# Asking for the sum so far three units ahead instead of two, in a mixture-of-experts tail

## The chip, the cores and the metric

The kernel runs on one core of one Trainium2 chip. The time is device microseconds of that core; the median of several runs is compared. Below, PE is the tensor engine, DVE the vector engine, ACT the scalar engine, POOL the GpSimd engine, SP the sync engine. Matrix results land in PSUM, everything else that the engines work on lies in SBUF, and the large tensors lie in DRAM.

## The reference

Four residual blocks on 4096 tokens (4 x 1024) of width 1024, each gated by a tanh of an input: a block-quantized projection of the context, an 8-bit/ternary linear layer, an 8-head attention over feature blocks, and a mixture of eight low-rank experts. The change lies in the last block:

```python
norm = jnp.maximum(jnp.linalg.norm(x, axis=-1, keepdims=True), 1e-12)
routing_weights = softmax(x / norm @ router_w)            # 8 experts
rw, selected_experts = jax.lax.top_k(routing_weights, 2)
rw = rw / jnp.sum(rw, axis=-1, keepdims=True)
combine = sum(one_hot(selected_experts, 8) * rw[..., None], axis=1)
for e in range(8):
    out = out + combine[:, e, None] * (x @ Wa[e] @ Wb[e])  # 1024 -> 128 -> 1024
x = x + tanh(g_ffn[1]) * out                               # x inside is the layer norm of x
```

So each token gets two expert terms, one from the lower-numbered and one from the higher-numbered of its two experts, on top of its own row.

## The kernel before

Up to about 1660 us the kernel computes the first three blocks and the routing, with the tokens in 32 tiles of 128. The last block works on another tiling. Tokens are sorted into lists by expert, once by the lower and once by the higher expert of each token, and every list is cut into **units** of 128 tokens of one expert (`class Unit`). There is room for 38 units of each kind (`NS` = 38, `NU` = 76): units 0 to 37 are those of the lower expert, units 38 to 75 those of the higher. Room is taken for the worst split of tokens over experts, so the last units of a list, and of each expert, hold padding. A padding row's index lies out of bounds, and such a row is not transferred.

A unit takes these steps:

- `gather` (POOL, L1395): an indirect DMA fetches the 128 rows of the unit, 1028 values each (the row, its two expert weights, and the scale and offset of its layer norm). Lower down this is called the row gather.
- `normalize` (ACT, L1414), `transpose` (PE L1431 into two PSUM tiles, ACT L1435 copies both out as hgT).
- `choose` and `fetch` (DVE, L1440, L1444, L1451): read the expert's number and copy its two weight matrices to fixed places of `arena["w"]`, two places for each matrix.
- `down` (PE L1460, then ACT L1465 copies the 128x128 result as ygT) and `up` (PE L1470, two halves of 512 into a PSUM tile of which there are two).
- `finish` (DVE, L1485): og = weight x product + base, and then `send` (POOL, L1495): an indirect DMA stores the 128 rows of og. For og there are three buffers.

For a unit of the lower expert, the base is the token's own row, and the store goes to a DRAM tensor `x4`. For a unit of the higher expert, the base is the **sum so far**, the rows that the lower half stored in `x4`; they are fetched by one more indirect DMA on POOL, `resume` (L1407), and og goes to the output. A token's two units can be anywhere, so the first `resume` has to wait until every store of the lower half has landed. Because of that, units 38 and 39 are "held": their `finish` writes only weight x product (L1482), and `settle` (L1491) adds the sum so far and stores when unit 40 is at its finish.

`resume` has four buffers, by the unit's number modulo 4: two of a pool's tag `vT` for remainders 0 and 1, and slots 2 and 3 of `arena["x"]` for the others.

Everything in this stage runs in the order in which it is written, on each engine separately (`manual_schedule` for PE, DVE, ACT and POOL). The loop at the end of the kernel issues, for unit s: row gathers that run up to 14 units ahead, `down` of s+1, `choose` and `transpose` of s+2, `normalize` of s+3, `fetch` of s+1, `up` and `finish` of s, and then `resume` of s+2. On each engine a unit's steady order is thus:

- PE: down s+1, transposes s+2, up s
- ACT: ygT s+1, two copies hgT s+2, normalize s+3
- DVE: first weight copy (s+2), second weight copy (s+1), og s
- POOL: row gather of s+14 (until unit 62, when there are no more rows to fetch), store s, resume s+2

SP issues nothing in this stage. All indirect DMAs go through one queue of POOL, and the eight counters that tell of their landing are used in turn.

Of the kernel before, what the change touches and what calls it, by code (L numbers as in the profile page):

```python
# [53 lines left out]
def flamingo_kernel(  # L54
# [63 lines left out]
    NS = (NTOK + (NE - 1) * (P - 1)) // P  # L118
    NU = 2 * NS
# [45 lines left out]
    with ExitStack() as s1:  # L165
# [79 lines left out]
        class Media(Fp8):  # L245
# [11 lines left out]
            def range(self):  # L257
                g = self.group
                nc.vector.tensor_reduce(
                    g.column(g.rmax, self), self.c.rearrange("p (b k) -> p b k", k=P), AX.X, ALU.max,  # L260
                    apply_absolute_value=True,
                )
                if self is g.tiles[-1]:
                    g.turn()
# [32 lines left out]
        class Group:  # L297
# [17 lines left out]
            def begin(self):  # L315
                self.rmax = self.tiny("rmax")
# [1183 lines left out]
    us = [Unit(s) for s in range(NU)]  # L1500
# [4 lines left out]
    def tail(before):  # L1505

        t = NT - 1
        listed, last = routes[t - 2], routes[t - 1]
        before.cross()
        for name in ("w", "x"):  # L1510
            arena[name] = w2.tile([P, 4, XW], F32, tag="sq", name=f"arena_{name}")

        nc.gpsimd.memset(arena["x"][:, 3, D - 12 : XW], 0.0)
        for i in (3, 7):
            nc.gpsimd.memset(eT_x[:, i, D - 12 : XW], 0.0)
        attended(t - 1, 1)
        last.moments()
        for u in us[3:6]:
            u.gather()
        attend(t, 0, 0)  # L1520
        listed.count()
        attend(t, 0, 1)
        last.normalize()
        listed.enlist()
        listed.send()
        attend(t, 0, 2)
        last.transpose(0)
        last.take(0)
        attend(t, 0, 3)
        last.transpose(1)  # L1530
        last.take(1)
        attended(t, 0)
        attend(t, 1, 0)
        last.logits()
        us[0].normalize()
        last.collect()
        attend(t, 1, 1)
        last.total()
        last.softmax()
        us[1].normalize()  # L1540
        last.choose()
        last.classify()
        us[6].gather()
        attend(t, 1, 2)
        attend(t, 1, 3)
        us[0].choose()
        us[1].choose()
        us[0].fetch()
        attended(t, 1)
        routes[t] = Route(t)  # L1550
        routes[t].moments()
        us[0].transpose()
        last.count()
        last.enlist()
        last.send()
        us[1].transpose()
        us[0].down()
        us[2].normalize()
        routes[t].normalize()

    def hooks(s):

        h = [nothing] * 4
        r = routes[NT - 1]
        if s == 0:
            h[3] = lambda: (r.transpose(0), r.take(0))
        elif s == 1:
            h[1] = lambda: (r.transpose(1), r.take(1))
            h[3] = lambda: (r.logits(), r.collect())
        elif s == 2:  # L1570
            h[1] = lambda: (r.total(), r.softmax())
            h[2] = r.choose
            h[3] = r.classify
        elif s == 3:
            h[1] = lambda: (r.count(), r.enlist(), r.send())
            h[2] = rest.measure
        elif s == 4:
            h[1] = rest.place
            h[3] = rest.find
        elif s == 6:  # L1580
            h[1] = rest.list
        return h
# [52 lines left out]
    with tc.manual_schedule(engines=ORDERED):  # L1635
        intro()
        for t in range(NT):
            for mb in range(NB):
                now = step(t, mb, now)
                e = (t - NT + 2) * NB + mb - 3  # L1640
                if 0 <= e < NE:
                    nc.sync.dma_start(wb_sb[:, e, :], wb[e])
                if t == NT - 1:
                    if mb == 2:
                        early.measure()
                    elif mb == 3:
                        early.place()
                    elif mb == 5:
                        early.find()
                    elif mb == 7:  # L1650
                        early.list()
                        for u in us[0:3]:
                            u.gather()
        tail(now)
        done = 7
        for s, u in enumerate(us):
            begin, first, second, end = hooks(s)
            begin()

            ahead = min(s + 7, EARLY) if s < 7 else min(s + 14, done + 2)  # L1660
            for a in us[done:ahead]:
                a.gather()
            done = max(done, min(ahead, NU))
            if s == NS:
                u.resume()
                us[s + 1].resume()
            if s + 1 < NU:
                us[s + 1].down()
            first()
            if s + 2 < NU:  # L1670
                us[s + 2].choose()
                us[s + 2].transpose()
            second()
            if s + 3 < NU:
                us[s + 3].normalize()
            if s + 1 < NU:
                us[s + 1].fetch()
            u.up()
            if s == NS + 2:
                us[NS].settle()  # L1680
                us[NS + 1].settle()
            u.finish()
            if NS <= s < NU - 2:
                us[s + 2].resume()
            end()


# [36 lines left out]
```

## Time and profile before

The median of three runs is 2027.59 us (2027.41 to 2028.21). The profile is one further execution.

| | |
|---|---|
| time of the profiled execution | 2021.54 us |
| its span, first to last instruction | 2019.8 us |
| mean granted TensorE clock | 0.987 |
| PE, DVE, ACT, POOL busy over the span | 1919.0, 1642.1, 1448.3, 598.9 us |
| units 0 to 37, from the first up-product | 1664.5 to 1840.1 us |
| units 38 to 75 | 1840.1 to 2014.4 us |
| one undisturbed unit on PE | 4.38 us |
| `resume` on POOL (38 of them) | 1.0 us each, median |
| `send` on POOL | 1.2 us each, median |
| og on DVE | 1.28 us each |

In a timeline each row is the start in us, the duration in us, engine, line, operation, what is written from what is read; the brackets at its end hold the time that the engine stood idle before, and what ended it. An indirect DMA's duration on POOL is that of its issue alone; the data lands later. "remote" is a release that the profile can't name. "issue" is time for which it shows no wait. PE's ends are modelled, so starts are compared here.

### The profile page before, as it was taken

The numbers are of one execution on the slowest core, as the hardware profiler recorded it, in microseconds if no ns is written. First come the engines' busy times: TensorE is split into PE (matmuls) and PEld (weight loads), VectorE is DVE, ScalarE is ACT, GpSimd is POOL, SyncE is SP. The second block draws the span as 40 slices with busy tenths as digits, with TensorE's granted clock in tenths as the row PEclk, the third lists the DMA queues.
The fourth block names the chain that finished last, engine by engine and source line by source line (L and its number), as shares of the span: only waits on it lengthen the run. The fifth ranks groups of instructions, "written<-read, shape, count | busy, mean of one in ns | idle before, by whom it ended". The sixth has DMA issues, their size and how long they took to land.

```text
span 2019.8 us, 25358 instructions
## 1 busy us (share of the span) xinstructions
PE 1919.0 (95%) x7379; PEld 1016.3 (50%) x7411; DVE 1642.1 (81%) x3381; ACT 1448.3 (72%) x2458; POOL 598.9 (30%) x915
## 2 busy tenths in 40 slices
PE   3899999999789999999999999999999989999998
PEld 3644444444334444444444444444444447777676
DVE  8799888866778999999999999999999856555555
ACT  8988888998567777777777777777777645555554
POOL 2232323344300212121211111111111136546664
PEclk9899999999899999999999999999999999999999
DMA  4243233252376777777777777777777856746885
GB/s 156 95 158 124 94 115 105 103 199 95 145 206 159 181 195 179 197 180 196 184 192 183 193 182 193 183 193 181 195 184 182 223 162 213 268 169 201 288 301 175
DMA packets 125328, 359.89 MB, mean 178 GB/s; under 512 B 30647, under 2 KB 38839, under 8 KB 125190
## 3 DMA queue, kind: packets, MB, share of 16 engines
q1 hardware_dynamic: 95670, 273.87, 49.6%
q0 software_dynamic: 29520, 84.39, 12.5%
q8 instruction: 60, 0.98, 0.2%
q14 instruction: 78, 0.64, 0.1%
HBM read 166.18 MB, written 75.61 MB: 120 GB/s over the span
## 4 chain that ended last, share of the span: by engine, by line
PE 82%; DVE 6%; ACT 4%; issue 4%; POOL 3%; DMA 1%; POOLq 0%; another core or an unknown queue 0%; DVEq 0%; ACTq 0%
PE av L994 21%; PE sc L914 21%; PE mm L427 18%; PE f L875 5%; PE dn L1460 5%; PE up L1470 4%; PE pt_hmT L1042 1%; PE ptx L414 1%; PE pt_hg_pt L1431 1%; PE pt_hg_acc L1431 1%; PE pq L1054 1%; ACT e L923 1%; DVE nmax L919 1%; POOL a_all L133 1%; PE ptq L867 1%
## 5 line engine op out<-in xcount | busy, mean ns | idle before, releaser
L914 PE MATMUL sc<-kv,q 128*128 128x512 f32 x1024 | 489.6, 601 | 3.9 <-ACT q L902 2.1
L994 PE MATMUL av<-eT_x,vT 128*128 128x512 f32 x1008 | 477.3, 596 | 2.3 <-issue 0.4
L923 ACT ACTIVATE e<-sc,nmax 128x1024 f32<-128x1024 f32 x256 | 285.1, 1113 | 229.1 <-DVE nmax L919 226.2
L427 PE MATMUL mm<-wq,hT 128*128 128x512 f32 x960 | 423.7, 598 | 6.1 <-DVE x1s L447 6.1
L919 DVE TENSOR_REDUCE nmax<-sc 128x1 f32<-128x1024 f32 x256 | 311.8, 1218 | 44.0 <-PE sc L914 43.8
L929 ACT ACTIVATE e<-e,rden 128x1024 f32<-128x1024 f32 x256 | 294.2, 1149 | 58.9 <-DVE rden L926 55.2
L942 DVE STREAM_TRANSPOSE sq<-e 128x1024 f32<-128x1024 f32 x252 | 310.8, 1233 | 0.1
L994 PEld LDWEIGHTS av<-eT_x,vT 128*128 128x128 f32 x1008 | 189.3, 190 | 231.3 <-issue 227.4
L427 PEld LDWEIGHTS mm<-wq,hT 128*128 128x128 f32 x960 | 180.5, 192 | 218.2 <-issue 205.0
L914 PEld LDWEIGHTS sc<-kv,q 128*128 128x128 f32 x1024 | 185.5, 191 | 188.0 <-issue 176.1
L1460 PEld LDWEIGHTS dn<-hgT,arena_w 128*128 128x128 f32 x1216 | 148.3, 193 | 50.2 <-issue 35.9
L1460 PE MATMUL dn<-hgT,arena_w 128*128 128x128 f32 x1216 | 151.5, 278 | 12.2 <-ACT hgT L1435 7.7
L133 POOL TENSOR_TENSOR rstd_c<-ve_c,neg_half 128x1 f32<-128x1 f32 x31 | 17.6, 568 | 461.8 <-DVE nrm L1069 405.2
L1470 PE MATMUL up<-arena_w,ygT 128*128 128x512 f32 x304 | 143.0, 593 | 0.0
L875 PE MATMUL f<-wb_sb 128*128 128x512 bf16 x465 | 115.4, 379 | 4.2 <-DVE y L883 1.4
L1465 ACT COPY ygT<-dn 128x128 f32<-128x128 f32 x76 | 20.1, 265 | 127.0 <-PE dn L1460 92.8
L225 ACT ACTIVATE y_x<-x,off_x,up_x 128x128 f32<-128x128 f32 x256 | 101.5, 480 | 1.1 <-POOL off_x L396 1.1
L237 ACT ACTIVATE hd<-q_x,down_x 128x128 f32<-128x128 bf16 x256 | 78.1, 388 | 26.2 <-DVE mu_a L363 17.5
L875 PEld LDWEIGHTS <-wb_sb 128*128 128x128 bf16 x496 | 48.5, 98 | 81.6 <-issue 29.7
L1144 POOL DMA_INDIRECT lists<-token,slot x64 | 66.6, 1041 | 67.6 <-DVE slot L1137 57.0
L133 POOL TENSOR_TENSOR y<-ve_d,neg_half 128x1 f32<-128x1 f32 x32 | 18.3, 572 | 213.4 <-issue 162.2
L133 POOL TENSOR_TENSOR a_all<-va,neg_half 128x1 f32<-128x1 f32 x32 | 46.9, 1465 | 97.9 <-DVE va L467 97.9
(297 smaller groups left out, 2940.9 us busy)
## 6 DMA issues: line engine op xcount, KB each, us to landing
eT_x<-sq SPq DMA_DIRECT2D x1008, 128.0 KB
x<-y SPq DMA_DIRECT2D x32, 514.0 KB
c<-in_ctx_t_dram SPq DMA_DIRECT2D x32, 512.0 KB
x<-in_x_dram SPq DMA_DIRECT2D x32, 512.0 KB
x<-x1s SPq DMA_DIRECT2D x32, 512.0 KB
y<-x SPq DMA_DIRECT2D x32, 512.0 KB
kv<-in_ctx_dram SPq DMA_DIRECT2D x32, 512.0 KB
vT<-in_ctx_t_dram SPq DMA_DIRECT2D x32, 512.0 KB
```

Source lines behind the costliest of these rows:

```text
L133: nc.gpsimd.tensor_tensor(dst, src, exponent, ALU.pow)
L225: nc.scalar.activation(self.y[:, cols(k)], src[:, cols(k)], AF.Identity, bias=bias[:, k : k + 1], scale=scale[:, k : k + 1],)
L427: nc.tensor.matmul(self.pm[:, hf * HALF : (hf + 1) * HALF], self.hT[:, k, :], wq[:, k, :], start=(k == 0), stop=(k == NB - 1),)
L875: nc.tensor.matmul(po, self.qT[:, k, :], w0T[:, k, cols], start=(k == 0), stop=(k == NB - 1),)
L914: nc.tensor.matmul(sc[:, halves(nh)], qs[t][:, mb * P : (mb + 1) * P], kv[:, halves(nh)], start=True, stop=True,)
L919: nc.vector.tensor_reduce(nmax, sc, AX.X, ALU.max, negate=True)
L923: nc.scalar.activation(self.e, sc, AF.Exp, bias=nmax, accum_out=self.den)
L929: nc.scalar.activation(self.e, self.e, AF.Copy, scale=self.rden)
L942: nc.vector.transpose(sq[:, :, :, j, :], self.e.rearrange("p (k q a) -> p q k a", k=NB, q=4))
L994: nc.tensor.matmul(out_ap, vTs[t][:, k, :], weights, start=(k == 0), stop=(k == NB - 1))
L1460: nc.tensor.matmul(po, self.wa[:, k, :], self.hT[:, k, :], start=(k == 0), stop=(k == NB - 1),)
L1470: nc.tensor.matmul(po[:, halves(hf)], self.yT, self.wb[:, halves(hf)], start=True, stop=True)
```

## The change

Each `resume` of the higher half is issued one unit sooner. Unit 38 begins with three of them (38, 39, 40), where it had two; after its finish comes 41. After unit 39 there is none. After unit 40, when `settle` has read the buffers of 38 and 39, come 42 and 43, and from then on unit s is followed by s+3. The buffers and their number stay the same, so in the steady state `resume` of s+3 fills the buffer that unit s−1 has read.

```diff
@@ the loop over units
             if s == NS:
-                u.resume()
-                us[s + 1].resume()
+                for a in us[s : s + 3]:
+                    a.resume()
             if s + 1 < NU:
                 us[s + 1].down()
             first()
@@
                 us[NS].settle()
                 us[NS + 1].settle()
             u.finish()
-            if NS <= s < NU - 2:
-                us[s + 2].resume()
+
+            for a in {NS: (3,), NS + 1: (), NS + 2: (2, 3)}.get(s, (3,) if s > NS else ()):
+                if s + a < NU:
+                    us[s + a].resume()
             end()
```

On POOL the order of instructions becomes, from unit 38 on (before: 38, 39, 40, row gather, 41, row gather, three stores, 42, row gather, store 41, 43, row gather, store 42, 44 and so on, where a bare number is a resume): 38, 39, 40, 41, two row gathers, stores of 38, 39 and 40, 42, 43, row gather, store 41, 44, row gather, store 42, 45 and so on. The number and the size of the DMAs are unchanged, and so are the orders of PE, DVE, ACT and SP.

## The prediction

> **What bounds the kernel now.** I read four views: the busy table by stage, the waits of the last stage, its timeline unit by unit, and the chain that ended last. The change touches only the second half of the expert stage (units 38 to 75), so the first question is how much time that half can give back.
>
> The busy table by stretches (us of the stretch; then busy us and instruction count of PE, PEld, DVE, ACT, POOL; then granted clock, DMA share, GB/s), cut where the higher expert's units begin (1840) and where the row gathers of its units run out (1966):
>
> ```profile
> core 0: us, PE busy (x) PEld busy (x) DVE busy (x) ACT busy (x) POOL busy (x), PEclk, DMA share, GB/s
> ...
> 1660.00:1840.00 180.00, 175.20 (x1136) 135.97 (x1135) 105.51 (x165) 98.67 (x162) 99.04 (x98) 1.00 0.61 205
> 1840.00:1966.00 126.00, 117.79 (x730) 89.99 (x729) 67.02 (x80) 65.48 (x104) 83.41 (x79) 0.99 0.83 281
> 1966.00:2020.00 54.00, 46.70 (x284) 34.88 (x282) 27.58 (x33) 23.62 (x39) 26.17 (x24) 0.97 0.53 179
> ```
>
> TensorE is busy 117.8 of 126 us even in the stretch with the heaviest DMA. A unit costs it 4.38 us: its up-products start at 1938.77, 1943.14 and 1947.52. Subtracting 4.376 us from every step between up-products of units 38 to 74 leaves 12.3 us lost, in three places. (a) Units 42 and 43: 0.80 + 5.27 us (up-products at 1853.23, 1858.41, 1868.06). (b) Units 50 and 53: 2.83 + 2.23 us (1894.32 to 1901.52; 1910.28 to 1916.88). (c) Units 62 to 64: 0.05 + 0.28 + 0.86 us. All other steps are 4.37 or 4.38. **12.3 us, 0.6% of the run, is all that can be won.**
>
> The waits of 1836 to 2020 (engine, line, what ended the wait: us in total, times, longest):
>
> ```profile
> ACT ygT L1465 <- PE dn L1460: 41.4, 27, 2.9
> ...
> DVE og L1485 <- PE up L1470: 34.1, 18, 4.4
> ...
> DVE og L1485 <- remote: 12.0, 3, 4.2
> ...
> DVE og L1485 <- DMA arena_x<-x,idx_rest: 9.6, 5, 3.0
> ...
> DVE og L1485 <- DMA to<-x,idx_rest: 5.8, 3, 2.8
> ```
>
> The last two rows are the change's target: the output step (og) waits 15.4 us, in 8 units, for the sum so far to land; part of the 12.0 us "remote" may be the same. But that is DVE's wait. Does it reach TensorE? Two units from the timeline (start, us, engine, line, what; in brackets the idle time before it):
>
> ```profile
> 1938.77 1.88 PE L1470 MATMUL up<-arena_w,ygT 128*128 128x512 f32 x4
> 1941.90 1.28 DVE L1485 SCALAR_TENSOR_TENSOR og<-up,xg,arena_x 128x1024 f32<-128x1024 f32 x1 [1.64 <-DMA arena_x<-x,idx_rest]
> 1943.14 1.88 PE L1470 MATMUL up<-arena_w,ygT 128*128 128x512 f32 x4
> 1947.52 1.88 PE L1470 MATMUL up<-arena_w,ygT 128*128 128x512 f32 x4
> ```
>
> Here og is late, 3.13 us after its up-product starts (1.92 in an undisturbed unit), and the next two up-products still come on the beat. The slack can be worked out. Behind og on DVE stand the two weight copies (0.68 us each); the first serves the down-product that starts 1.72 (up) + 1.78 (down) + 0.88 (transposes) + 1.72 (up) = 6.1 us after that up-product. og takes 1.28 us and the copy 0.68, with about 0.1 between, so og may start **about 4.0 us** after its up-product before TensorE feels it. Only units 49 (5.12), 60 (4.04), 61 (4.17) and 42 (4.74) are at or over that. For 61 it shows: its copy ends at 1957.95 and the down-product of unit 64 starts at 1958.10 instead of 1958.04. That is the 0.05 us.
>
> The large losses look different. Unit 49 to 50:
>
> ```profile
> 1891.41 1.01 POOL L1407 DMA_INDIRECT to<-x,idx_rest  x1 [0.30 <-issue]
> ...
> 1894.32 1.88 PE L1470 MATMUL up<-arena_w,ygT 128*128 128x512 f32 x4
> ...
> 1896.02 0.27 ACT L1465 COPY ygT<-dn 128x128 f32<-128x128 f32 x1 [3.53 <-PE pt_hg_acc L1431]
> ...
> 1897.45 0.59 ACT L1435 COPY hgT<-pt_hg_pt 128x512 f32<-128x512 f32 x1 [1.17 <-PE up L1470]
> 1898.09 0.97 PEld L1460 LDWEIGHTS dn<-hgT,arena_w 128*128 128x128 f32 x8 [2.72 <-ACT hgT L1435]
> ...
> 1898.82 0.58 ACT L1435 COPY hgT<-pt_hg_acc 128x512 f32<-128x512 f32 x1 [0.78 <-remote]
> ...
> 1899.43 1.28 DVE L1485 SCALAR_TENSOR_TENSOR og<-up,arena_x,to 128x1024 f32<-128x1024 f32 x1 [3.89 <-remote]
> ```
>
> og does wait (its gather was asked for at 1891.41, 8.0 us earlier), but TensorE stands still for ACT's copies of the transposes, and ACT stands still for TensorE's own finished products: ygT comes 4.36 us after its down-product starts (1891.66), against 2.04 in an undisturbed unit. That chain, TensorE to ACT to TensorE, has no sum-so-far in it. Unit 53 reads the same (3.72), unit 43 worse (7.39). So the losses fall where DMA is busiest, and two symptoms stand side by side there: og waits for data, and ACT sees TensorE's results late. The change treats the first.
>
> **The change, part by part.** *Start, unit 38.* The gather for unit 40 moves from after unit 38's finish to before its down-product. POOL already runs back to back there (1842.26, 1843.55, 1845.08, each 0.3 us after the last), so its place in the queue is the same; the gather for 41 overtakes one row gather (1847.66 to about 1846.4), which is needed 14 units later. Cost 0; nobody waits for either.
>
> *Unit 40.* POOL's queue was: store 38, store 39, store 40, gather 42, row gather, store 41. Now gather 43 is put in behind gather 42. It is one ask, 1.0 + 0.3 us of POOL: the row gather and store 41 go from 1856.81 and 1858.12 to about 1858.1 and 1859.4. Store 41 is next needed when its og buffer comes round, three units (13 us) later; it lands well before. Gather 43 itself comes 2.7 us earlier than its old 1859.52. Cost on the path 0; if the crowd of transfers is what holds ACT up at units 42 and 43, one ask more: 6.07 us over the eight asks of 1851 to 1861 is 0.8 us each. Bounds 0 to +0.8; I take 0, as the eight asks stay the same eight plus one that was due 2.7 us later.
>
> *Units 41 to 72.* Per unit POOL issues store s, gather s+3 (was s+2), row gather: the same three asks in the same order, 1.2 + 1.0 + 1.0 us and three gaps of 0.3 = 4.1 us of the 4.38. Bytes and asks are unchanged, and no wait is added: the buffer that gather s+3 fills was read by unit s−1's og, which ended a unit ago. DVE has behind og only its weight copies, and they come earlier. What is gained is lead: in an undisturbed unit a gather is asked for 5.68 us before og starts,
>
> ```profile
> 1993.09 1.01 POOL L1407 DMA_INDIRECT arena_x<-x,idx_rest  x1 [0.31 <-issue]
> ...
> 1998.77 1.28 DVE L1485 SCALAR_TENSOR_TENSOR og<-up,xg,arena_x 128x1024 f32<-128x1024 f32 x1 [1.89 <-PE up L1470]
> ```
>
> and 10.06 us with one unit more. How long does it need? The first one, from the chain that ended last:
>
> ```profile
> 1842.26 5.10 DMA arena_x<-x,idx_rest
> ```
>
> 5.1 us in light traffic, and up to 8.0 us at unit 49. So 5.68 is short in heavy traffic and 10.06 covers every case seen: the 15.4 us of DVE waits go, with most of the rest of og's lateness. The Trainium skill's rule (DMA: Bandwidth & Descriptors, Anatomy of one DMA, SWDGE path) speaks against the change: about 2.0 us fixed plus size over 436 GB/s, 3.2 us for these 524 KB, so two units ahead would always be enough and the waits removed would be zero. The rows say 5.1 to 8.0, since an ask queues behind others; I take the rows, so og does come on time. By the rule the sum is 0, by the rows it is what og's lateness costs TensorE: at least the 0.05 us of unit 62, at most all of (c), 1.19 us. The rows don't separate the two symptoms there; I take half, **−0.6 us**.
>
> A second rule of the same page (Specifications) bounds what can be hoped for: about 358 GB/s of HBM per core. Three transfers of 524 KB per 4.38 us would be 359. The trace has 305 GB/s at 88% DMA share over 1880 to 1960 (padding rows aren't moved), so the stage isn't bandwidth-bound by the row, and by the rule it nearly is; asking sooner adds no bandwidth under either.
>
> *End.* The last gathers are asked one unit sooner; the last units' og already follow their up-products (2012.82 after 0.51 idle on PE). 0.
>
> **Sum.** 0 + 0 − 0.6 + 0. The profiled execution has a span of 2019.8 and a time of 2021.54; it would become 2020.9. The median of the runs is 6.05 us above that execution; I carry the difference over: 2027.59 − 0.6 = **2027.0 us**. About 0.2% (4.1 us) is what a measurement of this kernel can tell from no change.
>
> **Rivals.** *Faster.* og's wait and ACT's late copies share a cause that the change relieves: at units 49 and 52 og's waits are at their longest where TensorE stops. Then (b) and (c) go: 2.83 + 2.23 + 1.19 = 6.3 us, 2021.3. If (a) goes too, 12.3 us, 2015.3. Against it: og comes 3.1 to 4.2 us after its up-product in units 57 to 61 and TensorE loses no more than the 0.05 us, and in (a) ACT is released at 1863.02, ahead of og at 1863.14, so og was not what held it.
>
> *Slower.* Late og is a brake: the store waits for og (POOL's stores wait 38.3 us for DVE, up to 3.3 at a time), and so do the asks behind it. With og on time the asks of units 44 to 62 come without pauses, at 88% DMA share already, and ACT's late-copy bubbles (2.2 to 2.8 us each, in units 50 and 53) come more often. Two more of them, 5.1 − 0.6 = +4.5 us, pass the 0.2%: 2032.1. For it: no such bubble after 1966, where asks per unit fall from three to two. Against: TensorE sets the mean rate of asks either way.
>
> *It doesn't do what it says.* POOL's asks carry landing counters that come round every eight asks, so an ask waits for the one eight before it. Eight asks are 2.7 units, 11.7 us, and the longest landing seen is 8.0, so this should not bite; if it does, og is as late as before: 2027.6.
>
> **How the numbers follow.** Waits removed off the path (2027.0): 0.55, its own range 2025 to 2029. No effect (2027.6): 0.04. Faster rival (2021.3, with a tail to 2015): 0.23. Slower rival (2032.1): 0.18. So faster by over 0.2% 0.23, within 0.59, slower 0.18. The range reaches into both rivals until about a tenth is left on each side: 2020.5 to 2032.5.
>
> **What would show it.** Right: og's waits for arena_x and to nearly gone (under 3 us of 15.4), og starting 1.92 us after its up-product in units 55 to 64, POOL's asks at the same pace, up-product steps of 4.38, and TensorE's losses at units 42 and 43 still there. Wrong: ygT's lateness (over 2.1 us after its down-product's start) vanishing along with og's waits, which is the faster rival, or showing up in units that had none, which is the slower one. If store 41 or the og of unit 42 is late, the insertion at unit 40 was costed too low.

## The result, and the profile after

In runs taken in turn on one chip, the changed kernel takes 2031.26 us (median of 20) and the kernel before 2027.62 us (median of 20). The medians are 3.6 us apart. The ratio on record, which isn't the quotient of the two medians (1.0018), is 1.0026 [1.0017, 1.0034], about 5.3 us more. By that ratio the change is slower, just past the 0.2% that the prediction called measurable. The time lies inside the predicted range, but on the side of the slower rival (2032.1) and not of the likeliest case (2027.0).

The profiled execution of the changed kernel took 2035.28 us (span 2033.5), against 2021.54 (2019.8) before. Not all of these 13.7 us belong to the change. Taking 4.376 us off every step between up-products, as the prediction did, gives what TensorE lost:

| profile | units 1–37 | units 38–43 | units 44–73 |
|---|---|---|---|
| before | 9.3 us | 6.1 us | 6.3 us |
| after | 15.4 us | 8.5 us | 12.9 us |

Units 1 to 37 run the same code in both kernels, so their 6.1 us tell how far two executions can lie apart. The other 9.0 us are in the units that the change touches. Even these overstate it: the profile of before is of an execution 6.1 us under its median, that of after of one 4.0 us over its own.

The busy table by stretches of the kernel after, with the columns that the prediction showed:

```profile
core 0: us, PE busy (x) PEld busy (x) DVE busy (x) ACT busy (x) POOL busy (x), PEclk, DMA share, GB/s
...
1660.00:1840.00 180.00, 173.56 (x1091) 134.32 (x1091) 101.28 (x160) 96.09 (x157) 96.39 (x96) 0.97 0.59 199
1840.00:1966.00 126.00, 113.85 (x687) 87.49 (x686) 62.98 (x75) 61.39 (x98) 79.77 (x75) 0.96 0.79 267
```

Between 1840 and 1966 TensorE is busy 113.85 us instead of 117.79, and the DMA share falls from 0.83 to 0.79. Every engine does less in these 126 us, DMA too, so bandwidth isn't what stops them. The granted clock is 0.96 instead of 0.99, but it doesn't explain the loss: the steps outside a few units are 4.38 us as before. The loss sits in units 42 (0.76), 43 (7.69), 48 (1.46), 51 (4.76), 56 (1.46), 59 (1.70), 62 (1.07) and 63 (2.33).

The waits of 1836 to 2035 in the kernel after (engine, line, what ended the wait: total us, times, longest):

```profile
DVE og L1485 <- PE up L1470: 55.4, 27, 5.4
...
DVE og L1485 <- remote: 27.6, 7, 5.7
...
PEld dn L1460 <- ACT hgT L1435: 12.6, 7, 5.7
...
ACT ygT L1465 <- PE up L1470: 11.9, 3, 4.9
PE dn L1460 <- ACT hgT L1435: 8.9, 3, 4.9
...
ACT ygT L1465 <- remote: 6.4, 1, 6.4
```

The two rows of the prediction's target, og waiting for `arena_x` and `to` (9.6 and 5.8 us), are gone altogether. The change did what it says, as a second pair of profiles, with almost complete records of what landed when, shows below. But og waits longer for TensorE's product (34.1 to 55.4 us), "remote" grows from 12.0 to 27.6, and TensorE's down-products wait longer for ACT's copies (PE's own row from 5.9 to 8.9 us). The unit with the second largest loss, unit 51, from the timeline of the kernel after (start, us, engine, line, what; in brackets the idle time before it):

```profile
1904.80 1.95 PE L1460 MATMUL dn<-hgT,arena_w 128*128 128x128 f32 x16
...
1907.46 1.88 PE L1470 MATMUL up<-arena_w,ygT 128*128 128x512 f32 x4
1908.18 1.00 POOL L1407 DMA_INDIRECT to<-x,idx_rest  x1 [0.31 <-issue]
1910.80 0.27 ACT L1465 COPY ygT<-dn 128x128 f32<-128x128 f32 x1 [4.88 <-PE up L1470]
1911.55 0.58 ACT L1435 COPY hgT<-pt_hg_pt 128x512 f32<-128x512 f32 x1 [0.48 <-remote]
1911.61 1.28 DVE L1485 SCALAR_TENSOR_TENSOR og<-up,eT_x,arena_x 128x1024 f32<-128x1024 f32 x1 [4.02 <-remote]
...
1912.19 3.07 PE L1460 MATMUL dn<-hgT,arena_w 128*128 128x128 f32 x16 [2.85 <-ACT hgT L1435]
```

Unit 50's sum so far was asked for at 1899.83, 11.8 us before og starts. The longest that any of these sums took to land, in the profiles that tell it, is 8.1 us, so data is hardly what og waits for. Unit 51's down-product started at 1904.80; its copy ygT starts at 1910.80, 6.00 us later, where 2.04 is usual. Unit 50's og starts 4.15 us after the up-product, where 1.92 is usual. The row of ygT says that TensorE ended the wait. (It names the up-product, TensorE's last instruction by the modelled ends; what ygT reads is the down-product.) Two engines that need different products of TensorE start within 0.8 us of each other. TensorE's signals that a product is finished come late (the last section says why this is put down to the signals), and TensorE then stands 2.85 us for the copies that ACT couldn't make earlier. This is the chain that the prediction found in units 43, 50 and 53 of the kernel before, and it has grown. The number of late ygT (over 2.2 us after their down-product) in units 44 to 73 stays at 9; the longest goes from 4.36 to 6.00 us.

### The profile page after: what moved, and what is told of

Its sections match the earlier page's. It is cut to its first block, busy times and chain, and to the rows that moved or that the text cites. A ratio compares the mean times of both kernels' runs of the same rounds, so it can differ in the third digit from the quotient of the medians.

```text
span 2033.5 us, 25357 instructions
## 1 busy us (share of the span) xinstructions
PE 1924.8 (95%) x7379; PEld 1021.8 (50%) x7411; DVE 1641.8 (81%) x3381; ACT 1448.7 (71%) x2458; POOL 599.0 (29%) x915
## 4 chain that ended last, share of the span: by engine, by line
PE 79%; issue 6%; DVE 6%; POOL 5%; ACT 3%; DMA 0%; POOLq 0%; DVEq 0%; ACTq 0%
PE av L994 21%; PE sc L914 21%; PE mm L427 17%; PE f L875 5%; PE dn L1460 3%; PE up L1470 3%; PE pt_hmT L1042 1%; PE ptx L414 1%; PE pq L1054 1%; POOL arena_x L1407 1%; POOL a_all L133 1%; ACT e L923 1%; POOL to L1407 1%; DVE nmax L919 1%; POOL out_dram L1495 1%
## 5 line engine op out<-in xcount | busy, mean ns | idle before, releaser
L237 ACT ACTIVATE hd<-q_x,down_x 128x128 f32<-128x128 bf16 x256 | 78.1, 387 | 26.5 <-DVE mu_a L363 17.8
```

## Experiments

The kernels below ran in six sets, each set on one chip together with the kernel before. That kernel took 2012.2 to 2013.3 us in sets 1, 2 and 5, and 2026.0 to 2026.7 in sets 3, 4 and 6. The profiles say what parts the two groups: in the first, ygT starts 2.04 to 2.12 us after its down-product in every unit of 38 to 73 (two profiles have one late unit each); in the second it is late in 6 to 17 units of every kernel that has its row gathers. The text calls these the *quiet* sets and the *late* sets. The first comparison above was a late one. What a theory said for one group often failed in the other, and that turned out to be the finding.

By the chip numbers on record, sets 1 and 5 ran on chip 6, sets 2 and 6 on chip 1, set 3 on chip 0 and set 4 on chip 15; the first comparison has no number. Set 2 was quiet, and set 6, half an hour later, was late. If the number means the same chip both times, being quiet or late is not a lasting property of a chip.

A second thing parts the groups. Of the DMA issues between 1836 and 2020 us (what is written from what is read, times, median us from issue to landing), a quiet profile of the kernel before (`before_2`) and the late one of the first comparison say:

```profile
arena_x<-x,idx_rest POOLq DMA_INDIRECT x22, 5.3
to<-x,idx_rest POOLq DMA_INDIRECT x18, 5.3
```

```profile
arena_x<-x,idx_rest POOLq DMA_INDIRECT x22
to<-x,idx_rest POOLq DMA_INDIRECT x18
```

Every quiet profile has times to landing, and no late one has any, because part of the records is missing there. In a late profile, then, the name of what ended a wait is less sure, above all "remote" and the absence of a DMA row.

### One part alone: the double ask, or the steady lead (set 1, quiet)

`burst` keeps the three asks at unit 38 and the two at unit 40, then goes back to two units ahead. `steady` starts as before and goes to three ahead at unit 44.

```diff
-            if NS <= s < NU - 2:
-                us[s + 2].resume()
+            asks = {NS: (3,), NS + 1: (), NS + 2: (2, 3), NS + 3: ()}
+            for a in asks.get(s, (2,) if s > NS else ()):
+                if s + a < NU:
+                    us[s + a].resume()
```

```diff
-                u.resume()
-                us[s + 1].resume()
+                for a in us[s : s + 2]:
+                    a.resume()
...
+            for a in (2, 3) if s == NS + 6 else (2,) if NS <= s < NS + 6 else (3,) if s > NS else ():
+                if s + a < NU:
+                    us[s + a].resume()
```

> Only the start of the change: three resumes ahead of unit 38's down-product, 41 after unit 38, 42 and 43 together after unit 40, none after unit 41; from unit 42 on two ahead as before. Theory 'lead' (the steady lead of three keeps the DMA queue full and multiplies the late-signal bubbles): within 1.5 us of before, 2027.6. Rival 'crowd' (one ask more in the crowd of transfers at unit 40 lengthens the bubble at units 42 and 43): all of the loss, about 2031, with a bubble at unit 43 of 7 us or more against 5.3.

> Only the steady part: units 38 to 43 as before, two resumes (46 and 47) after unit 44, then three ahead to the end. Theory 'lead': most of the loss, about 2031, bubble at unit 43 as before (5 to 6 us) and more lost time in units 46 to 64 than the 6 to 7 us of before. Rival 'crowd': as before, 2027.6.

Measured against before's 2012.24: `burst` 2013.04, ratio 1.0006 [0.9997, 1.0015]; `steady` 2006.45, ratio 0.9971 [0.9961, 0.9981]. The steady lead alone is a gain here, and the double ask does nothing measurable. So a part of a change that had just measured slower is faster by itself, in another set.

### Fewer row gathers in the crowded stretch (set 1, quiet)

`before_spread` and `after_spread` hand out the row gathers of the second half later: at most one per unit, and none in eight units (40, 41, 44, 48 and every fourth after).

```diff
             ahead = min(s + 7, EARLY) if s < 7 else min(s + 14, done + 2)
+            if s >= NS:
+                ahead = done if s - NS in (2, 3, 6, 10, 14, 18, 22, 26) else min(s + 14, done + 1)
```

> The kernel before (two ahead), with the 24 row gathers of the higher half spread over 32 units instead of 24: none after units 40, 41, 44, 48, 52, 56, 60 and 64, otherwise one per unit. Same bytes in all. Theory 'full queue' (TensorE's finished signals reach ACT late only while the DMA queue has no gaps): fewer bubbles, 3 to 8 us faster than before, 2020 to 2025. Rival (the bubbles come from something else than DMA load, such as the wait of og): no change, 2027.6.

> The changed kernel (three ahead) with the same spread of row gathers. Theory 'full queue': the loss of the change goes with the bubbles, within 1.5 us of the spread kernel with two ahead. Rival 'lead for another reason than a full queue': the 3.6 to 5 us between the two kernels stay.

Measured: `before_spread` 2011.35, ratio 1.0000 [0.9991, 1.0009]; `after_spread` 2005.22, ratio 0.9972 [0.9960, 0.9984]. In this set the gain comes with the lead, not with the spreading. A second set (5, quiet) put `before_spread` at 0.9991 [0.9982, 1.0000].

> Two ahead with the row gathers spread. On a chip with late signals, theory 'deeper queue': 2 to 8 us faster than before, since fewer transfers stand in the queue and late og is rarer; rival 'spread helps only the lead of three': as before. On a quiet chip: as before (2012), as on the other.

### The changed kernel itself in a quiet set, no row gathers, and the kernel before (sets 2 and 5)

> The changed kernel itself once more, beside the kernel before on this call's chip. In the four runs before, the kernel before took 2012.2 us instead of 2027.6, and no ygT came late. Theory 'two effects' (the lead of three removes what late og costs TensorE, some 6 us, and where ACT sees TensorE's results late under a full DMA queue it adds bubbles): where the kernel before takes about 2012 us, 5 to 7 us faster than it; where it takes about 2027 us, 3 to 6 us slower, as in the first comparison. Rival 'crowd at unit 40': slower than the steady part alone by 3 us or more on either.

> The steady part alone, again, to stand beside the whole change on one chip. Theory 'two effects': within 1.5 us of the whole change on this chip, whichever sign that has. Rival 'crowd at unit 40': 3 us or more faster than the whole change.

`before_nogather` and `after_nogather` leave the row gathers of units 52 to 75 out; those units compute with rows that were fetched earlier.

```diff
             s, j = self.s, self.j % 16
+            if s >= NS + 14:
+                self.x = eT_x[:, j % 6, :]
+                self.to = self.x[:, 0:D]
+                return
```

> Two ahead, but units 52 to 75 fetch no rows of their own: they take what an earlier unit left in the buffers, so those 24 row gathers are left out, and the values of these units are other tokens'. Two transfers per unit instead of three in the whole higher half. Theory 'full queue': late og and late ygT both vanish but for the crowd at units 40 to 43, and the higher half loses under 6 us (12.3 in the first profile), under 1 us where ygT is never late. Rival (late signals have nothing to do with DMA load): losses as before.

> Three ahead with the same row gathers left out (the values of units 52 to 75 are other tokens'). With no full queue the lead has nothing to remove and nothing to add: within 1 us of the two-ahead kernel without these gathers. Rival 'lead costs by itself': 3 us or more slower than it.

Measured against 2013.26: the changed kernel 2006.17, ratio **0.9964 [0.9951, 0.9977]**; `steady` 2006.37, 0.9966 [0.9953, 0.9978]; `before_nogather` 2004.72, 0.9961 [0.9948, 0.9973]; `after_nogather` 2005.55, 0.9960 [0.9945, 0.9975]. So the very change that cost 0.26% in the first comparison gains 0.36% in this set. Without row gathers, two and three units ahead are alike: the gain is the removal of something that needs three transfers per unit.

What it is, a profile of the kernel before in a quiet set shows (set 5, one execution, 2010.27 us).

> The kernel before, unchanged, for a profile on this call's chip. If it is a quiet chip (near 2013 us), theory 'late og costs TensorE where og starts over 4 us after its up-product': ygT at 2.04 us throughout, og 4 us and later in the units before each lost step, 6 to 8 us lost in units 44 to 73. If not, as the first profile: 12 us lost in the higher half, about half of it in units 44 to 73.

Its timeline around unit 47:

```profile
1868.17 1.02 POOL L1407 DMA_INDIRECT arena_x<-x,idx_rest  x1 [0.30 <-issue]
...
1870.37 1.88 PE L1470 MATMUL up<-arena_w,ygT 128*128 128x512 f32 x4
...
1874.13 0.27 ACT L1465 COPY ygT<-dn 128x128 f32<-128x128 f32 x1 [1.73 <-PE dn L1460]
1874.75 1.88 PE L1470 MATMUL up<-arena_w,ygT 128*128 128x512 f32 x4
1875.60 1.28 DVE L1485 SCALAR_TENSOR_TENSOR og<-up,eT_x,arena_x 128x1024 f32<-128x1024 f32 x1 [3.21 <-PE pt_hg_acc L1431]
1876.80 0.68 DVE L1444 COPY arena_w<-wa_sb 128x1024 f32 x1
...
1877.63 2.02 PE L1460 MATMUL dn<-hgT,arena_w 128*128 128x128 f32 x16 [1.00 <-DVE arena_w L1444]
...
1879.44 1.28 DVE L1485 SCALAR_TENSOR_TENSOR og<-up,eT_x,arena_x 128x1024 f32<-128x1024 f32 x1 [1.35 <-DMA arena_x<-x,idx_rest]
...
1880.36 1.88 PE L1470 MATMUL up<-arena_w,ygT 128*128 128x512 f32 x4
```

ygT is on time. The sum of unit 46 was asked for at 1868.17 and landed 7.3 us later, just before its og starts, 5.22 us after its up-product (1870.37); the transpose that the row of og names had long ended. The weight copy behind it ends at 1877.48, the down-product that needs this copy starts 0.15 us later after 1.00 us of standing, and the next up-product comes after 5.61 us instead of 4.38. The next og waits for its sum to land. In this profile og starts over 4.0 us after its up-product in 11 units of 44 to 73, and units 44 to 73 lose 5.8 us, 5.5 of it in steps behind such an og. In the changed kernel in a quiet set (set 2) no og of 44 to 73 is that late and the loss is 0.0:

```profile
1840.00:1966.00 126.00, 126.00 (x807) 98.27 (x805) 73.63 (x90) 71.81 (x116) 95.05 (x85) 1.00 0.89 315
```

TensorE is busy in all of the 126 us, at a DMA share of 0.89. These two profiles have almost all landings, so their waits of 1836 to 2020 test what the change was for. `before_2`, then `after_2`:

```profile
DVE og L1485 <- DMA arena_x<-x,idx_rest: 9.7, 6, 2.0
DVE og L1485 <- DMA to<-x,idx_rest: 7.7, 4, 2.3
```

```profile
DVE og L1485 <- DMA to<-x,idx_rest: 2.4, 1, 2.4
DVE og L1485 <- DMA arena_x<-x,idx_rest: 2.0, 1, 2.0
```

The waits for sums fall from 17.4 us in 10 units to 4.4 in two. Why two units ahead are too few can be read from the same profiles. With og on time the ask for a sum comes 8.75 us ahead of its og where row gathers are still issued (units 55 to 60 of the changed kernel), here for unit 57:

```profile
1913.46 1.02 POOL L1407 DMA_INDIRECT to<-x,idx_rest  x1 [0.31 <-issue]
...
1922.21 1.28 DVE L1485 SCALAR_TENSOR_TENSOR og<-up,xg,to 128x1024 f32<-128x1024 f32 x1 [1.89 <-PE up L1470]
```

One unit less would be 4.38 us. In the kernel before the sums asked for between 1858 and 1959, among row gathers, take 5.4 us (`to`) and 6.2 us (`arena_x`) to land, in the median; those asked for between 1962.5 and 1994, without row gathers, take 4.5. So among row gathers og comes late; the store behind it comes late, and the ask behind the store.

### More traffic on purpose (set 3, late)

If late og is a brake on the asks, then a kernel that keeps it should bear more DMA than one without it. `before_loaded` and `after_loaded` write half of each og of units 42 to 63 once more, to a scratch tensor, from SP (262 KB per unit).

```diff
             u.finish()
+            if s >= NS + 4 and s < NS + 26:
+                nc.sync.dma_start(x1_dram[s - NS][:, 0:HALF], u.o[:, 0:HALF])
```

> Two ahead, with more DMA load on purpose: for the units 42 to 63 the first half of og's columns is also copied to an unused DRAM tensor (262 KB per unit, through SP's queue; the output is untouched). Demand in the stretch goes from three transfers of 524 KB per unit to three and a half, over what the queue moved at its best. Theory 'a full queue alone makes TensorE's signals late': ygT comes 2.3 us and more after its down-product's start in several units even on a chip where it never does, and the higher half loses 20 us or more. Rival 'late signals belong to some chips only': on such a chip ygT stays at 2.04 us, and what is lost comes from og alone.

> Three ahead with the same added copies. Theory 'the lead helps until signals come late, and then hurts': if ygT comes late under this load, slower than the loaded kernel with two ahead by 2 us or more; if not, faster than it by 3 us or more. Rival 'under a full queue the lead is indifferent, since DMA sets the pace': within 2 us of it.

Measured against 2026.66: `before_loaded` 2026.13, ratio 0.9999 [0.9987, 1.0010]; `after_loaded` 2029.51, ratio 1.0017 [1.0006, 1.0028]. The same stretch of `before_loaded`:

```profile
1840.00:1966.00 126.00, 117.98 (x738) 88.46 (x737) 65.85 (x80) 65.04 (x105) 84.75 (x78) 1.00 0.92 324
```

and of `after_loaded`:

```profile
1840.00:1966.00 126.00, 112.53 (x673) 86.73 (x672) 62.86 (x75) 60.76 (x97) 80.47 (x75) 0.95 0.89 314
```

The kernel with two units ahead moves 324 GB/s and keeps TensorE busier than the other does at 314. Unit by unit, `before_loaded` has og 3.95 to 5.80 us late in units 51 to 62 and loses 0.1 to 0.9 us in each of them, 6.1 us together, while ygT is on time there (2.11) in all but one. `after_loaded` has og on time between bubbles, 10 late ygT, and single losses of 4.03 (unit 56) and 4.82 us (unit 62). Its loss of 44 to 73 is 13.2 us, against 7.0. So by these two profiles the kernel pays in this set either in many small steps for late og, or in few large ones for late products, and the large ones are dearer. The two profiles overstate by how much: that of `before_loaded` is of its fastest execution (2021.90 us), and the medians are 3.4 us apart. With two units ahead the extra traffic by itself cost nothing measurable, and the 20 us of loss that a full queue alone was expected to bring came to 11.6 in the profile (units 38 to 73).

### Parts of the change in a late set (set 4), and a brake put back (sets 5 and 6)

> Only the start of the change (42 and 43 asked for together after unit 40, two ahead from then on). So far two chips gave the changed kernel 0.36% less than the kernel before or its steady part 0.3% less, and one chip (the first comparison) 0.26% more. On a chip where ygT comes late (the kernel before near 2027 us), theory 'deeper queue' (three ahead lets more transfers stand in the queue, and there TensorE's signals come late): within 2 us of before. Rival 'crowd at unit 40': all of the loss, 3 us or more slower than before. On a quiet chip (before near 2013): as before, within 1.5 us.

> Only the steady part (units 38 to 43 as before, from 44 on three ahead). On a chip with late signals, theory 'deeper queue': 2 us or more slower than before; rival 'crowd at unit 40': as before or faster. On a quiet chip: 6 us faster than before, as on the other two.

> Three ahead, row gathers of the higher half spread over 32 units with none after units 40 and 41. On a chip with late signals, theory 'deeper queue': the queue empties in the units without a row gather, bubbles shrink, 5 us or more faster than the changed kernel, so 2026 us or less. Rival 'the lead makes signals late whatever stands in the queue': as the changed kernel, 2030 to 2031. On a quiet chip: 2005 to 2006.

> Three ahead without the row gathers of units 52 to 75 (those units' values are other tokens'). On a chip with late signals, theory 'deeper queue': none of the late ygT after unit 45, higher half loses under 8 us, so about 2019 to 2022. Rival as for the spread kernel: 2030. On a quiet chip: 2005, as before on one.

`braked` has the lead of three but makes POOL read the buffer of unit s+1 before the ask for s+3, for s = 41 to 62. POOL then stands until that sum has landed, so at most two sums are on their way at once.

```diff
                 if s + a < NU:
+                    if NS + 2 < s < NS + 25:
+                        w = us[s + 1].to
+                        stop = small.tile([P, 2], F32, tag="kept", name=f"stop_{s}")
+                        nc.gpsimd.tensor_tensor(stop, w[:, 0:2], w[:, 2:4], ALU.add)
                     us[s + a].resume()
```

> Three ahead with a brake on POOL: from unit 41 to 62, before resume s+3 POOL adds four landed values of the sum for unit s+1 (0.2 us), so it asks no further until that gather, asked for two units before, has landed. og need not wait for it, but the queue can't grow deeper. On a chip with late signals (before near 2027): theory 'deeper queue': as before or faster, 2027 or less, instead of 2031; rival 'the lead itself makes signals late': 2030 to 2032. On a quiet chip: within 2 us of the changed kernel, 2005 to 2008, if POOL's 0.25 us per unit suffice for the added instruction; slower if not.

> The braked kernel once more; on a quiet chip it took 2008.6 us beside 2013.1. On a chip with late signals (before near 2027): theory 'deeper queue': as before or faster, 2027 or less, instead of about 2031, and fewer microseconds lost in units 44 to 73 than the 13 to 18 of the unbraked kernels; rival 'the lead itself makes signals late': 2030 to 2032.

What was measured in late sets (the first comparison for `before` and `after`, set 6 for `braked`, set 4 for the others), with TensorE's loss from one profile of each kernel (us):

| kernel | ratio to before | units 38–43 | units 44–73 | longest ygT of 44–73 |
|---|---|---|---|---|
| before | 1 | 6.1 | 6.3 | 4.36 |
| after | 1.0026 [1.0017, 1.0034] | 8.5 | 12.9 | 6.00 |
| `burst` | 0.9997 [0.9986, 1.0008] | 6.2 | 9.0 | 5.31 |
| `steady` | 1.0024 [1.0013, 1.0036] | 6.3 | 17.8 | 7.43 |
| `braked` | 1.0018 [1.0004, 1.0032] | 8.4 | 9.9 | 5.95 |
| `after_spread` | 0.9988 [0.9975, 1.0001] | 0.0 | 13.7 | 5.99 |
| `after_nogather` | 0.9920 [0.9904, 0.9936] | 0.0 | 2.0 | 4.82 |

Four readings follow. First, the loss is in the steady lead: `steady` without the double ask is as slow as the whole change, and `burst` with it is not slower. With the loaded kernels counted in, three profiles with two units ahead lose 6.3 to 9.0 us in units 44 to 73, and five with three ahead lose 9.9 to 17.8. Second, three transfers per unit are needed for it: with the row gathers gone, the changed kernel takes 2010.41 us against 2026.04, and its stretch is almost that of a quiet set:

```profile
1840.00:1966.00 126.00, 124.33 (x795) 96.88 (x794) 72.86 (x88) 70.67 (x115) 67.41 (x61) 1.00 0.65 218
```

Third, the crowd at units 42 and 43 can be taken out by itself: `after_spread` skips the row gathers of units 40 and 41, and the 8.5 us of units 38 to 43 become 0.0. Its later losses stay. Fourth, `braked` was to bring the time back to before's 2027 and did not (2029.36). Its interval leaves out 1 and holds the 1.0026 of the whole change, so how much the brake helped, if at all, isn't shown: its bubbles of 44 to 73 come to 9.9 us in one profile, less than those of the unbraked kernels, one of them 5.4 us (unit 62), and units 48 to 51 lose 0.2 us each with ygT at 3.67 to 3.78. In the quiet set 5 it measured 2008.55, ratio 0.9971 [0.9960, 0.9982], a gain like that of the lead without it, with no loss in units 38 to 73. A cap of two on the sums under way therefore doesn't undo the change. Whether it is the earlier start of the asks as such that makes TensorE's signals come later, or the pauses that late og makes between them, isn't settled.

`after_spread` is the version to keep: 0.9972 in a quiet set, and 0.9988 with an interval that just reaches 1 in a late one. It was slower in neither of its two sets. What the lead adds to it in a late set is open, since `before_spread` never ran in one.

## Why the prediction was wrong, step by step

**Start, unit 38 (0).** Held. No unit of 38 to 40 loses anything in the profile after.

**Unit 40 (0, bounds 0 to +0.8).** As part of the total it was right: `burst`, which has the double ask, measured 0.9997 in a late set and 1.0006 in a quiet one. In the profiles of units 42 and 43, though, the upper bound was too low: the three kernels that ask for 43 early and go on with three ahead lose 8.3 to 8.5 us there in late sets, the others 4.6 to 6.3, with the spread and gather-free kernels, which lose none, aside. That is 2 to 4 us, in single profiles. `steady` is as slow without it, so it doesn't carry the result.

**Units 41 to 72 (−0.6).** This is the step that failed, and within it the term for ACT's late copies, which was put at nothing. Its first half held: og's waits for `arena_x` and `to` went from 15.4 us to none, and the lead in undisturbed units without row gathers is 10.06 us, as worked out. The rest failed in two ways.

- *The size of og's lateness.* The lead of 5.68 us was read from a unit near 1993, where POOL issues two asks per unit. Where it issues three, the lead with og on time is a unit less than 8.75, so 4.38, and no gather of 5.1 us makes that. Late og was therefore the rule in the stretch and not a matter of four units. The slack of "about 4.0 us" was right: the profile of the kernel before in a quiet set loses 5.5 of its 5.8 us behind og that are later than that. Where nothing else is late the change gains 7 us (0.9964), of which those 5.8 are seen in the profile. That is a little more than the 6.3 of the faster rival but by a different route: that rival wanted ACT's late copies cured, and there are none in units 38 to 73 of that set. Two readings behind this term were off without changing it. The 8.0 us at unit 49 are the time until og started, not a landing. And the late down-product of unit 64 stands between the up-products of 62 and 63, so its delay of 0.06 us is part of the 0.28 of unit 63 and not the 0.05 of unit 62. The profile of before had only three such og in units 44 to 73, since TensorE stood for other reasons in the same stretch.
- *The cost of og on time.* The step took ACT's late copies as unaffected by the lead, because bytes and asks are unchanged. In the late sets they aren't unaffected: TensorE stands longer behind its own late signals and loses 12.9 us in units 44 to 73 instead of 6.3 in the first comparison, and the steady lead alone made the time 1.0024 of before's in set 4 (2031.25 us against 2026.04). "TensorE sets the mean rate of asks either way", held against the slower rival, is true of the mean and says nothing of how long a bubble lasts.

**The two page figures.** The sums landed after 4.5 us in the median without row gathers and after 5.4 and 6.2 us among them, so the estimate of 3.2 us from the Trainium skill's fit (DMA: Bandwidth & Descriptors, Anatomy of one DMA, SWDGE path) is too short for an ask that has others beside it, and two units ahead did not do. The 358 GB/s of the same page (Specifications) were not reached: the quiet set ran at 315 GB/s with TensorE fully busy, and the loaded kernel at 324.

**The rivals.** *Slower* was the right one in direction and size: +4.5 predicted, 3.6 measured by the medians and 5.3 by the ratio, with bubbles in the place it named. Its wording was "more often"; the profile has the same number of late ygT (9) and longer ones. That late og spares the kernel larger losses is supported by `before_loaded` against `after_loaded`, and put in doubt as the whole story by `braked`. *Faster* is what the same kernel does in a quiet set. *It doesn't do what it says* is excluded by the waits that vanished, from 17.4 us to 4.4 where landings are on record.

**What would show it.** og's waits: right. og at 1.92 us in units 55 to 64: wrong in the first comparison (3.88 to 4.74 in units 55, 58, 61 and 62; the rows say "remote", but the trace has a signal of TensorE 0.02 us ahead of each of the four starts), right in a quiet set. The losses of units 42 and 43 still there: right, and larger. The sign that unit 40 was costed too low, a late og of unit 42, came true: 6.21 us after its up-product, against 4.74 before. The sign named for the slower rival, late ygT in units that had none, came true in units 48, 52, 55 and 56; units 51, 59 and 63, late before, became later (2.62, 2.92 and 2.49 us to 6.00, 4.59 and 6.00), and units 50, 53, 54 and 64 came to be on time. With one execution on each side, which units are late tells little. The one profile and three times of before couldn't tell how much this stage would differ from set to set; the prediction had treated 2027.59 and its losses as the kernel's own.

## What to carry to other kernels

Read a lead from a stretch that has the same number of asks per unit as the one you change: one more ask per unit took 1.3 us from the lead here and made landings 0.9 to 1.7 us longer, and that decided whether a transfer was late. When a wait for data is removed and another wait stands beside it in the same units, the second one has to be costed with the first gone; here it was the dearer one. And repeat a change of some tenths of a per cent in more than one set, on another chip and at another time, before keeping it: this one is 0.26% slower or 0.36% faster with the same code.

## What the hardware showed that was not expected

- The same kernel takes 2012 to 2013 us in three sets and 2026 to 2028 in three others and in the first comparison. Most of the difference is in this stage: the first up-product starts at 1662.0 to 1664.5 us in every profile, quiet or late, and of the 11.3 us between the two profiles of the kernel before, 2.1 lie ahead of it. With three indirect DMAs per 4.38 us, ACT and DVE start on TensorE's finished products up to 8.16 us after a down-product's start in some sets, and at 2.04 us in others, at similar or higher DMA rates (315 GB/s in the quiet set against 267). What makes a set one or the other isn't known from these runs.
- With row gathers left out, the late set loses its lateness too, but for one unit (2010.41 us). The lateness is thus tied to the transfers, but not to their bytes alone: `before_loaded` moved more bytes in the stretch (324 GB/s) with fewer late products (3 in units 44 to 73, against 9 before, in single profiles).
- It is TensorE's signals that are late, and they come in packs at a pace of their own. In the kernel after (units 58 to 60), TensorE starts its products on the beat, and their four readers on ACT and DVE then start about 0.7 us apart:

```profile
1946.03 1.95 PE L1460 MATMUL dn<-hgT,arena_w 128*128 128x128 f32 x16
...
1947.81 0.60 PE L1431 MATMUL pt_hg_pt<-ident,hg 128*128 128x128 f32 x4
...
1948.25 0.60 PE L1431 MATMUL pt_hg_acc<-ident,hg 128*128 128x128 f32 x4
...
1948.69 1.88 PE L1470 MATMUL up<-arena_w,ygT 128*128 128x512 f32 x4
...
1950.62 0.27 ACT L1465 COPY ygT<-dn 128x128 f32<-128x128 f32 x1 [3.50 <-PE up L1470]
...
1951.35 0.58 ACT L1435 COPY hgT<-pt_hg_pt 128x512 f32<-128x512 f32 x1 [0.47 <-PE up L1470]
...
1952.05 0.59 ACT L1435 COPY hgT<-pt_hg_acc 128x512 f32<-128x512 f32 x1
...
1952.79 1.28 DVE L1485 SCALAR_TENSOR_TENSOR og<-up,xg,arena_x 128x1024 f32<-128x1024 f32 x1 [3.47 <-remote]
```

  The trace has TensorE's four signals at 1950.54, 1951.28, 1952.03 and 1952.77, 0.75 us apart. By the modelled ends the products were finished 0.43, 0.44 and 1.72 us apart, the last at 1950.57. Steps of 0.72 to 0.78 us between TensorE's signals don't occur in units 38 to 73 of any quiet profile; the late profiles have 7 to 27 of them, and the late one without row gathers has 2. What holds the signals up, and why the lead makes the packs longer, isn't known.
